# A graph layer with gathered rows: a fifth buffer for rows of x, loaded one stage earlier, paid for by two smaller tiles

## The chip, the cores and the metric

The kernel runs on one core of one Trainium2 chip. The metric is device time in microseconds (us), as the median of several runs. Beside the timed runs there is one execution under the hardware profiler; all engine times, waits and orders in time come from that one.

## The reference

One layer of a graph network over N = 8192 nodes with C = 256 features and E = 131072 edges, sorted by destination:

```
ea   = edge_attr @ w_e + b_e
agg  = segment_sum(relu(x[src] + ea), dst, N)
h_local = bn1(relu((x + agg) @ w1 + b1) @ w2 + b2 + x)
h_attn  = bn2(attention within groups of 32 nodes, 4 heads, out_w + x)
out  = h_local + h_attn
out  = bn3(out + relu(out @ m_w1 + m_b1) @ m_w2 + m_b2)
x    = layernorm(x + out)
```

## The kernel before, in words

**Edges.** The edges are cut into 128 blocks of 1024. For each block POOL issues eight indirect gathers (`gather`, L212 to L228), each of 128 rows of x or, from block 20 on, of xb, a copy of x with b_e added. They land in a tile xs, of which there are six (BUFS). For eight blocks the last gather is replaced by single row loads on SP (`row_stream`, L243, tile xf), so there are 1016 gathers. DVE transposes the edge attributes (eaT, L304), TensorE (PE) multiplies them with w_e (tile pe), DVE adds pe to xs (L363), ACT applies relu in place (L367). DVE builds a one-hot matrix oh from the offsets rel of the edges' destinations within their group (`edge_hot`, L375). PE sums the messages by group with it (tile pw, `pair_sums`), ACT copies a pair's sums to ws (`edge_sums`, L411), and PE places them by a second one-hot oh2 into a window of node columns (tile l, `edge_place`), which DVE adds to xT (L437).

**Nodes.** The 8192 nodes are 16 chunks of 512. A chunk goes through three generators:

- `attention_front` (L583): load the rows of x (`load_nodes`, L442 to L444, tile xn, four buffers), transpose them on PE (L178), copy them to xT and a scaled form to hA on ACT (L594, L595), and make q and k (at<-xT,inT; ACT L608 evacuates).
- `attention_back` (L612): v, the scores, softmax, and the output projection (L690).
- `dense` (L696): two layers on x + agg (w1 with L716, w2 with L720), two more layers on the sum (mw1 with L727, mw2 with L740), then transposes back (zT, L748), the residual with the rows of xn (L754), statistics and normalisation (L756 to L766), and the store (L771). The residual is the last reader of xn.

A front of chunk c may begin when the dense stage of chunk c - 4 has set "dense" (L761), that is, when its rstd is issued. The front first issues its load and yields LOAD, which makes the planner let that stream rest (two turns in the early part, FAR = 10 planned us later on), and only then records the transposes.

**The order.** PE's order is written out by a planner in the kernel: the class `Work` holds four streams (two dense streams, fronts, backs) and hands out pieces of them between edge pieces, by planned times in us. Up to block NV = 24 (`stated`) the orders of DVE and ACT are written out too; behind that the tile framework orders them. SP issues its DMAs in its own order: edge attributes (L267, four buffers), row loads, xn loads, stores. A stage of the back stream sets `after`, and `may` (L892) lets the stream go on only when enough messages have been told; `told` is counted only while `stated` holds.

**The holds.** `hold_fetches` (L189) ties every gather to a PE instruction: gather n waits for the last PE instruction whose planned time is at most n x 1.254 - 10 us, so that gathers don't run ahead of the work.

Of the kernel before, what the change touches and what calls it, by code (L numbers as in the profile page):

```python
# [9 lines left out]
FP = mybir.dt.float32  # L10
I32 = mybir.dt.int32
BF = mybir.dt.bfloat16
# [7 lines left out]
P = 128  # L20
N, C, E, ED, H, NPG = 8192, 256, 131072, 64, 4, 32
# [3 lines left out]
NB = E // BE  # L25
# [3 lines left out]
TB = NH * TJ  # L29
# [5 lines left out]
CH = 512  # L35
NCH = N // CH
BPC = NB // NCH
TN = CH // P
# [42 lines left out]
def window(b):  # L81
    return NPB + 2 * SLACK[b]
# [6 lines left out]
def gnn_kernel(ctx: ExitStack, tc: tile.TileContext, x, src, dst, edge_attr, w, out):  # L89
    nc = tc.nc  # L90

    const = ctx.enter_context(tc.tile_pool(name="const", bufs=1))
# [22 lines left out]
    agg = dram.tile([AGG_ROWS, C], FP, name="agg")  # L115

    srci = const.tile([P, NB, TB], I32, name="srci")
    rel = const.tile([P, NB, TB], FP, name="rel")
    wrow = const.tile([P, NB], FP, name="wrow")
    width = const.tile([1, 1], I32, name="width")  # L120
    we = const.tile([P, C], FP, name="we")
# [30 lines left out]
    epool = fast.enter_context(tc.tile_pool(name="edge", bufs=1))  # L152
# [10 lines left out]
    clock, placed_at = [0.0], [-10.0]  # L163
# [218 lines left out]
    def group_sums(pw, i, b, turns):  # L382
        clock[0] += 0.13 * len(turns)
        for h, j in turns:
            matmul(
                pw[h * WN : (h + 1) * WN, i, :], oh_of[b][:, h * TJ + j, :], msg_of[b][:, h, j, :],
                start=(j == 0), stop=(j == TJ - 1), skip_group_check=True,
            )
# [13 lines left out]
    def edge_sums(blocks):  # L402

        n = len(blocks)
        pw = pw_of.pop(blocks[0], None)
        if pw is None:
            pw = pps.tile([P, 2, C], FP, name="pw", tag="at", bufs=4)
            for i, b in enumerate(blocks):
                group_sums(pw, i, b, [(h, j) for j in range(TJ) for h in range(NH)])
        ws = epool.tile([P, 2, C], FP, name="ws", tag="ws", bufs=2)  # L410
        newest["ws"] = nc.scalar.copy(ws[:, :n], pw[:, :n]).ins  # L411
        oh2 = epool.tile([P, 2, WB], FP, name="oh2", tag="oh2")
        for i, b in enumerate(blocks):
            wn = window(b)
            nc.vector.tensor_scalar(oh2[:, i, :wn], iota_n[:, :wn], wrow[:, b : b + 1], None, ALU.is_equal)
        return blocks, ws, oh2
# [20 lines left out]
            newest["xT"] = nc.vector.tensor_add(xT, l2[:, :, a - n : z - n], xT).ins  # L437

    chunk = [{} for _ in range(NCH)]
    stated = [True]  # L440

    def load_nodes(n0, st, pool):  # L442
        xn = st["xn"] = pool.tile([P, TN, C], FP, name="xn", tag="xn", bufs=4)
        nc.sync.dma_start(xn, x[ds(n0, CH), :].rearrange("(t p) c -> p t c", p=P))  # L444

    with tc.tile_pool(name="setup", bufs=1) as sp:
# [249 lines left out]
    def dense(n0, st, pool, bank, a=0, z=CH, own=("h1", "m1", "zT", "y", "")):  # L696
# [22 lines left out]
        for o in range(KC):  # L719
# [2 lines left out]
            ).ins  # L722
            yield 1.7 * part
        yield NEED
        m1 = pool.tile([P, 2 * KC, w], FP, name="m1", tag=own[1])
        for o in range(2 * KC):
            newest["relu"] = nc.scalar.activation(m1[:, o, :], layer(mw1, KC, o, hA), AF.Relu, bias=v_("m_b1", o)).ins  # L727
# [148 lines left out]
    class Work:  # L876
# [14 lines left out]

        def may(self, i):  # L892
            s = self.streams[i]
            return s and not self.rest[i] and self.told >= self.after[i] and clock[0] >= self.free[i] and s[0][0]()

        def run(self, us):
            self.owed += us
# [57 lines left out]
    with tc.manual_schedule(engines={PE}):  # L955
# [9 lines left out]
        for c in range(NCH):  # L965
            st, before, same = chunk[c], chunk[c - 1], chunk[c - 4]
# [50 lines left out]
        while b < TAIL:  # L1017
# [6 lines left out]
            for i in blocks:  # L1024
                if i + 2 < NB:
                    gather(i + 2)
                if 4 <= i < 8:
                    wt, name = ((w1, "w1"), (w2, "w2"), (mw1, "m_w1"), (mw2, "m_w2"))[i - 4]
# [13 lines left out]
            if stated[0]:  # L1042
# [8 lines left out]
                if waiting:  # L1051
                    pair_sums(1, waiting)
                    sums = edge_sums(waiting)
# [16 lines left out]
            else:  # L1070
                pair_sums(0, waiting)
                edge_products(b)
                pair_sums(1, waiting)
                sums = edge_sums(waiting)
                waiting = list(blocks)
                edge_messages(b)
# [17 lines left out]
        t, l, s = came[b - 2] + 20, b - 2, b - 2  # L1094
# [11 lines left out]
        while l < NB:  # L1106
# [56 lines left out]
            elif t >= times[2]:  # L1163
                i, k = p
# [11 lines left out]
        work.finish()  # L1176
    hold_fetches()
    fast.close()


    wide = nc.values_load(width[0:1, 0:1])
    with tc.If(wide > 0):
        with tc.tile_pool(name="gen", bufs=1) as pool, tc.tile_pool(name="gen_ps", bufs=1, space=PSUM) as ps_pool:
# [11 lines left out]
            with tc.For_i(0, E, P * TE) as e0:  # L1195
# [16 lines left out]
                for j in range(TE):  # L1212
# [17 lines left out]
                    ws = pool.tile([P, C], FP, name="gws", bufs=2)  # L1230
# [19 lines left out]
        with tc.tile_pool(name="gfin", bufs=1) as pool, tc.tile_pool(name="gfin_ps", bufs=1, space=PSUM) as ps_pool:  # L1250
# [7 lines left out]
            with tc.For_i(0, N, CH) as n0:  # L1258
                st = {}
# [42 lines left out]
```

## Time and profile before

| | us |
|---|---|
| median of 3 runs | 1316.11 |
| lowest, highest | 1313.69, 1318.36 |
| the profiled execution's own time | 1310.89 |
| its span, first to last instruction | 1309.1 |
| busy: PE, DVE, ACT, POOL | 1172.2, 800.4, 589.3, 969.2 |
| mean granted PE clock | 0.969 of full speed |
| HBM traffic over the span | 182 GB/s |

A group of instructions has its line, engine, operation, output <- inputs, the count, busy us and mean ns, and the idle time of the engine just ahead of it with what ended that. A timeline row has start and duration in us, engine, line, operation, tiles and count, and in brackets the idle time before it and its releaser. "SPq" is the queue of DMAs that SP issues. A row of waits has the waiter, whom it waited for, the total us, how often, and the longest. A row of windows has the stretch, the busy us of PE, PEld, DVE, ACT and POOL in it (with counts), the granted PE clock, the share of DMA time and GB/s. Matmuls are pipelined and their ends are modelled; an f32 matmul counts as two instructions in the trace and as one in an order.

### The profile page before, as it was taken

The numbers are of one execution on the slowest core, as the hardware profiler recorded it, in microseconds if no ns is written. First come the engines' busy times: TensorE is split into PE (matmuls) and PEld (weight loads), VectorE is DVE, ScalarE is ACT, GpSimd is POOL, SyncE is SP. The second block draws the span as 40 slices with busy tenths as digits, with TensorE's granted clock in tenths as the row PEclk, the third lists the DMA queues.
The fourth block names the chain that finished last, engine by engine and source line by source line (L and its number), as shares of the span: only waits on it lengthen the run. The fifth ranks groups of instructions, "written<-read, shape, count | busy, mean of one in ns | idle before, by whom it ended". The sixth has DMA issues, their size and how long they took to land.

```text
span 1309.1 us, 25348 instructions
## 1 busy us (share of the span) xinstructions
PE 1172.2 (90%) x7591; PEld 698.7 (53%) x7591; DVE 800.4 (61%) x1653; ACT 589.3 (45%) x842; POOL 969.2 (74%) x1024
## 2 busy tenths in 40 slices
PE   4969889899998899879997799899989898999886
PEld 3546455456554555445554455555545455555565
DVE  6676674568664765536667275675646575586653
ACT  2535343455535454344544345454444454543433
POOL 6777777677777777777777777777777777777772
PEclk8999989899999999989999799999999999999999
DMA  8999986758566666565755666676766766666641
GB/s 231 263 332 276 297 233 154 183 148 230 149 167 181 170 185 160 154 186 156 199 160 155 188 171 183 161 201 156 187 175 170 183 171 190 160 175 161 178 118 55
DMA packets 150762, 240.68 MB, mean 184 GB/s; under 512 B 28862, under 2 KB 114268, under 8 KB 149852
## 3 DMA queue, kind: packets, MB, share of 16 engines
q0 software_dynamic: 48768, 133.23, 38.4%
q1 hardware_dynamic: 100764, 105.77, 29.9%
q8 instruction: 62, 1.02, 0.3%
q14 instruction: 80, 0.66, 0.2%
q10 hardware_dynamic: 1088, 0.00, 0.0%
HBM read 222.13 MB, written 16.78 MB: 182 GB/s over the span
## 4 chain that ended last, share of the span: by engine, by line
PE 58%; DMA 15%; issue 8%; DVE 8%; POOL 5%; SPq 3%; ACT 3%; DVEq 0%; ACTq 0%; POOLq 0%
PE at L174 31%; PE pe L174 13%; DMA xs<-xb,srci 8%; PE pw L174 7%; POOL xs L221 5%; PE l L174 3%; DMA ea<-in_edge_attr_dram 3%; DVE xs L363 3%; DMA xn<-in_x_dram 2%; DMA xs<-in_x_dram,srci 1%; SPq L243 1%; SPq L267 1%; DVE bd L666 1%; PE at L797 1%; DVE eaT L304 1%
## 5 line engine op out<-in xcount | busy, mean ns | idle before, releaser
L221 POOL DMA_INDIRECT xs<-xb,srci x856 | 811.8, 948 | 265.0 <-issue 180.1
L367 ACT ACTIVATE xs<-xs 128x1024 f32<-128x1024 f32 (+1 forms) x251 | 261.9, 1046 | 386.6 <-DVE xs L363 355.6
L363 DVE TENSOR_TENSOR xs<-pe,xs 128x1024 f32<-128x1024 f32 (+1 forms) x251 | 296.6, 1205 | 155.1 <-PE pe L174 73.1
L174 PE MATMUL pe<-we,eaT 64*128 64x256 f32 x2048 | 274.0, 402 | 41.9 <-DVE xs L363 31.5
L174 PEld LDWEIGHTS pe<-we,eaT 64*128 64x128 f32 x2048 | 190.6, 192 | 130.5 <-DVE xs L363 42.3
L221 POOL DMA_INDIRECT xs<-in_x_dram,srci x144 | 140.0, 972 | 45.0 <-issue 28.6
L174 PE MATMUL pw<-xs,oh 128*32 128x256 f32 x2048 | 139.1, 391 | 1.6 <-ACT xs L367 1.6
L174 PE MATMUL at<-xT,inT 128*128 128x512 f32 x256 | 125.1, 620 | 9.1 <-DVE hA L720 6.7
L375 DVE TENSOR_TENSOR oh<-iota_n,rel 128x128 f32<-128x128 f32 x256 | 62.4, 280 | 99.7 <-PE pw L174 99.5
L174 PE MATMUL at<-hA,mw 128*128 128x512 f32 (+1 forms) x256 | 115.4, 578 | 0.0
L174 PE MATMUL at<-m,mw 128*128 128x512 f32 (+1 forms) x256 | 110.0, 574 | 2.4 <-DVE xT L437 1.6
L304 DVE STREAM_TRANSPOSE eaT<-ea 128x512 f32<-128x512 f32 x128 | 89.5, 700 | 16.7 <-PE pe L174 13.3
L174 PEld LDWEIGHTS pw<-xs,oh 128*32 128x32 f32 x2048 | 55.7, 110 | 78.6 <-issue 42.6
L174 PEld LDWEIGHTS l<-oh,ws 128*128 128x128 f32 x512 | 72.6, 190 | 33.1 <-issue 20.8
L174 PE MATMUL l<-oh,ws 128*128 128x160 f32 (+4 forms) x512 | 81.6, 298 | 5.3 <-DVE hA L690 3.4
L174 PEld LDWEIGHTS at<-xT,inT 128*128 128x128 f32 x256 | 47.9, 195 | 66.4 <-issue 49.2
L174 PEld LDWEIGHTS at<-m,mw 128*128 128x128 f32 x256 | 47.2, 191 | 52.1 <-issue 48.3
L727 ACT ACTIVATE m<-at,vec 128x512 f32<-128x512 f32 (+1 forms) x64 | 41.7, 656 | 69.1 <-PE at L174 69.0
L174 PEld LDWEIGHTS at<-hA,mw 128*128 128x128 f32 x256 | 46.4, 192 | 44.8 <-issue 37.4
L174 PE MATMUL at<-xT,w 128*128 128x512 f32 (+1 forms) x128 | 59.0, 593 | 9.7 <-DVE xT L437 9.7
L608 ACT ACTIVATE qk<-at,vec 128x512 f32<-128x512 f32 x64 | 43.5, 683 | 50.4 <-PE at L174 49.6
L174 PE MATMUL at<-oT,outT 128*128 128x512 f32 x128 | 61.2, 602 | 2.9 <-ACT oT L681 2.9
(163 smaller groups left out, 1216.4 us busy)
## 6 DMA issues: line engine op xcount, KB each, us to landing
ea<-in_edge_attr_dram SPq DMA_DIRECT2D x512, 128.0 KB
xf<-xb SPq DMA_DIRECT2D x1024, 1.0 KB
xs<-xb,srci POOLq DMA_INDIRECT x856
xn<-in_x_dram SPq DMA_DIRECT2D x16, 512.0 KB
out_dram<-y SPq DMA_DIRECT2D x14, 512.0 KB
xp<-in_x_dram SPq DMA_DIRECT2D x10, 512.0 KB
xb<-xp SPq DMA_DIRECT2D x10, 512.0 KB
xp<-in_x_dram SPq DMA_DIRECT2D x3, 1024.0 KB
```

Source lines behind the costliest of these rows:

```text
L174: mark(ps, nc.tensor.matmul(ps, *args, **kw).ins)
L221: nc.gpsimd.indirect_dma_start(out=xs[:, h, j, :], out_offset=None, in_=x if b < NX else xb[:, :], in_offset=bass.IndirectOffsetOnAxis(ap= ...
L243: nc.sync.dma_start(xf[m * QR + r : m * QR + r + 1, :], xb[ds(row, 1), :])
L267: nc.sync.dma_start(ea[p0 : p0 + QR, c0 : c0 + NH * EQ * ED].rearrange("r (g d) -> r g d", g=NH), edge_attr[b * BE : (b + 1) * BE, :].rear ...
L304: nc.vector.transpose(eaT, ea[:, QR:].rearrange("p (g d) -> p g d", d=ED)[:, :, :QR])
L363: nc.vector.tensor_add(msg[:, hs, js].rearrange("p u i c -> p i u c"), pe[:, js, u : u + n, :], xs[:, hs, js].rearrange("p u i c -> p i u c"),
L367: nc.scalar.activation(msg[:, hs, js], msg[:, hs, js], AF.Relu)
L375: nc.vector.tensor_tensor(oh[:, ts], iota_n[:, None, :WN].to_broadcast([P, TB // 2, WN]), rel[:, b, ts, None].to_broadcast([P, TB // 2, WN ...
L608: nc.scalar.activation(qk[:, o, :], ps, AF.Identity, bias=v_("in_b", o))
L666: nc.vector.transpose(bd[q, :, :, g, :].rearrange("p t h q -> p (t h) q"), pr3[q])
L727: newest["relu"] = nc.scalar.activation(m1[:, o, :], layer(mw1, KC, o, hA), AF.Relu, bias=v_("m_b1", o)).ins
L797: nc.tensor.matmul(ps[i], wt[:, k, o * P : (o + 1) * P], act[:, k, :], start=(k == 0), stop=(k == nk - 1))
```

## The change

It has four parts:

1. xn has five buffers instead of four. The load for chunk c + 4 is issued in the dense stage of chunk c, between the second and the third layer, in the whole-chunk stages of the fast path only. A front whose xn is there already neither loads nor yields LOAD.
2. rel is bf16 instead of f32 (2 KB instead of 4 KB a partition). It holds small whole numbers.
3. ws has one buffer instead of two (2 KB less a partition).
4. In `may`, the condition on `told` holds only while `stated` does.

```diff
-    rel = const.tile([P, NB, TB], FP, name="rel")
+    rel = const.tile([P, NB, TB], BF, name="rel")
...
-        ws = epool.tile([P, 2, C], FP, name="ws", tag="ws", bufs=2)
+        ws = epool.tile([P, 2, C], FP, name="ws", tag="ws")
...
-    stated = [True]
+    stated, fast_path = [True], [True]
...
-        xn = st["xn"] = pool.tile([P, TN, C], FP, name="xn", tag="xn", bufs=4)
+        xn = st["xn"] = pool.tile([P, TN, C], FP, name="xn", tag="xn", bufs=5)
...
         yield NEED
+        if fast_path[0] and not a and n0 // CH + 4 < NCH:
+            load_nodes(n0 + 4 * CH, chunk[n0 // CH + 4], pool)
         m1 = pool.tile([P, 2 * KC, w], FP, name="m1", tag=own[1])
...
-            return s and not self.rest[i] and self.told >= self.after[i] and clock[0] >= self.free[i] and s[0][0]()
+            return s and not self.rest[i] and (self.told >= self.after[i] or not stated[0]) and clock[0] >= self.free[i] and s[0][0]()
...
     fast.close()
+    fast_path[0] = False
```

The planner's decisions move with it. Three places show how. In the rows, at is a PSUM bank of the node work, l that of the placement, pe the edge products, pw the group sums; w_88 is w1, w_89 w2, h_... the tile h1. Lines behind L724 are two higher in the changed kernel.

First place: PE, at the end of chunk 0's dense stage (zT), the start of chunk 1's (w_88) and the front of chunk 4 (xn, inT). Before:

```order
L748 MATMUL at<-ident,zT 128x128 x8
L174 MATMUL l_2006<-oh_1942,ws 128x144 x4
L174 MATMUL at<-xT,w_88 128x512 x2
L178 MATMUL at<-ident,xn 128x128 x8
L174 MATMUL at<-xT,w_88 128x512 x2
L174 MATMUL at<-xT,inT 128x512 x2
L174 MATMUL at<-h_2013,w_89 128x512 x2
L174 MATMUL at<-xT,inT 128x512 x2
L174 MATMUL pe<-we,eaT 128x256 x8
```

Now:

```order
L750 MATMUL at<-ident,zT 128x128 x8
L178 MATMUL at<-ident,xn 128x128 x8
L174 MATMUL l_2016<-oh_1944,ws 128x144 x4
L174 MATMUL at<-xT,inT 128x512 x2
L174 MATMUL at<-xT,w_88 128x512 x2
L174 MATMUL at<-xT,inT 128x512 x2
L174 MATMUL at<-xT,w_88 128x512 x2
L174 MATMUL at<-xT,inT 128x512 x2
L174 MATMUL pe<-we,eaT 128x256 x8
```

The transposes of xn moved ahead of the placement, and a pair for q and k ahead of the first dense layer; the second layer (w_89) moved behind the edge products. On DVE, at the same place, the two additions to xT (L437) moved ahead of the reciprocal and the four scalings of y.

Second place: ACT, at the normalisation of chunk 7 and the front of chunk 11 (rstd is the reciprocal deviation's root, xT and hA the front's two copies). Before:

```order
L760 ACT_TABLE_LOAD
L760 ACTIVATE rstd<-mv,eps_t 128x4
L367 ACTIVATE xs<-xs 128x1024
L716 ACTIVATE h_7998<-at,vec 128x512 x2
L367 ACTIVATE xs<-xs 128x1024
L411 COPY ws<-pw 128x512
L360 ACTIVATE xs<-xs 128x1024
L594 COPY xT<-at 128x512
L595 ACTIVATE hA<-xT,cA,s_99 128x512
L594 COPY xT<-at 128x512
```

Now:

```order
L762 ACT_TABLE_LOAD
L762 ACTIVATE rstd<-mv,eps_t 128x4
L594 COPY xT<-at 128x512
L595 ACTIVATE hA<-xT,cA,s_99 128x512
L594 COPY xT<-at 128x512
L595 ACTIVATE hA<-xT,cA,s_99 128x512
L608 ACTIVATE qk<-at,vec 128x512
```

The copies of xT moved directly behind rstd; four rows of edge messages and of the dense layer that stood between moved behind them.

Third place: PE at the front of the same chunk 11. Before:

```order
L178 MATMUL at<-ident,xn 128x128 x8
L174 MATMUL pe<-we,eaT 128x256 x8
L174 MATMUL at<-h_7998,w_89 128x512 x2
L174 MATMUL at<-xT,inT 128x512 x2
L174 MATMUL at<-h_7998,w_89 128x512 x2
L174 MATMUL l_8205<-oh_8097,ws 128x160 x4
```

Now:

```order
L174 MATMUL pe<-we,eaT 128x256 x8
L750 MATMUL at<-ident,zT 128x128 x8
L178 MATMUL at<-ident,xn 128x128 x8
L174 MATMUL l_7995<-oh_7842,ws 128x160 x4
L174 MATMUL at<-xT,inT 128x512 x2
L174 MATMUL at<-xT,w_88 128x512 x2
L174 MATMUL at<-xT,inT 128x512 x2
```

The transposes of z and of xn stand back to back now, and only one placement is left between xn and the first pair for q and k, where edge products and a dense pair stood.

## The prediction

> **What bounds the kernel now.** I read the profile's page first, for the engines' shares and the slices.
>
> ```profile
> span 1309.1 us, 25348 instructions
> PE 1172.2 (90%) x7591; PEld 698.7 (53%) x7591; DVE 800.4 (61%) x1653; ACT 589.3 (45%) x842; POOL 969.2 (74%) x1024
> POOL 6777777677777777777777777777777777777772
> ...
> PE 58%; DMA 15%; issue 8%; DVE 8%; POOL 5%; SPq 3%; ACT 3%; DVEq 0%; ACTq 0%; POOLq 0%
> ```
>
> TensorE (PE) is the busiest, and the chain of the page goes through it for 58%. But the line to look at is the even row of sevens: POOL issues gathers at one rate from the start to the end. So I read the groups by line next, and then POOL's own timeline, gather by gather.
>
> ```profile
> L221 POOL DMA_INDIRECT xs<-xb,srci x856 | 811.8, 948 | 265.0 <-issue 180.1 <-PE at L174 23.2 <-PE pw L174 15.9
> L221 POOL DMA_INDIRECT xs<-in_x_dram,srci x144 | 140.0, 972 | 45.0 <-issue 28.6 <-DMA xs<-in_x_dram,srci 4.6 <-PE at L174 3.5
> 4.88 1.10 POOL L221 DMA_INDIRECT xs<-in_x_dram,srcd  x1 [3.28 <-issue]
> ...
> 136.59 0.94 POOL L221 DMA_INDIRECT xs<-in_x_dram,srci  x1 [0.67 <-DMA xs<-in_x_dram,srci]
> ...
> 150.65 0.95 POOL L221 DMA_INDIRECT xs<-in_x_dram,srci  x1 [1.09 <-PE at L174]
> ...
> 238.86 0.94 POOL L221 DMA_INDIRECT xs<-xb,srci  x1 [0.30 <-issue]
> 242.00 0.94 POOL L221 DMA_INDIRECT xs<-xb,srci  x1 [2.20 <-PE at L174]
> 245.49 0.94 POOL L221 DMA_INDIRECT xs<-xb,srci  x1 [2.55 <-ACT hA L595]
> 246.74 0.95 POOL L221 DMA_INDIRECT xs<-xb,srci  x1 [0.30 <-issue]
> ...
> 1286.77 0.94 POOL L221 DMA_INDIRECT xs<-xb,srci  x1 [0.30 <-issue]
> ```
>
> The fence's timeline rows give start, duration and, in brackets, the idle time before and its releaser. A gather takes 0.95 us and the next starts 0.30 us later whatever is named in the bracket, so a step is 1.25 us. From the first start (4.88) to the last (1286.77) there are 1015 steps, 1281.9 us, and 1015 x 1.25 = 1268.8. The 13.1 us over are gathers longer than 0.95 (the two groups' means of 948 and 972 hold them) and exactly four gaps above 0.30 in the whole run, the four shown: 0.37 + 0.79 + 1.90 + 2.25 = 5.3 us. What follows the last gather's start takes 1309.1 - 1286.77 = 22.3 us. So the time is 4.9 + 1281.9 + 22.3, POOL sets it, and an edit pays only if it shortens a gather's step, one of the four gaps, or the last 22.3 us. PE time by itself is worth nothing, unless PE is so late that a gather's hold (the PE instruction that it must wait for) has not been reached.
>
> Then the waits on x rows, the thing the change is about: the view of tile xn, and PE's and SP's timeline where PE waits longest.
>
> ```profile
>   DMA xn<-in_x_dram: 43.6, 7
> ...
> PE pe L174 <- DVE xs L363: 31.8, 17, 5.3
> PE at L178 <- DMA xn<-in_x_dram: 22.1, 4, 13.8
> ...
> 721.19 1.55 SPq L243 DMA_DIRECT2D xf<-xb  x4
> 722.84 0.40 SPq L444 DMA_DIRECT2D xn<-in_x_dram  x1
> ...
> 727.73 1.97 PE L178 MATMUL at<-ident,xn 128*128 128x128 f32 x8 [13.83 <-DMA xn<-in_x_dram]
> ...
> 569.96 1.97 PE L178 MATMUL at<-ident,xn 128*128 128x128 f32 x8 [6.06 <-DMA xn<-in_x_dram]
> ...
> 700.00:750.00 50.00, 35.02 (x174) 19.12 (x171) 21.50 (x41) 20.13 (x26) 37.80 (x41) 0.83 0.64 173
> 752.67 1.88 PE L174 MATMUL at<-hA,mw 128*128 128x512 f32 x4
> ...
> 755.46 0.94 POOL L221 DMA_INDIRECT xs<-xb,srci  x1 [0.30 <-PE pw L174]
> ```
>
> The first row counts PE's and its weight load's wait for xn (43.6), the third PE's alone: 22.1 us in four waits. PE's largest wait is another, 31.8 us for the edge messages of DVE. SP issues its queue in order, and the xn load stands behind edge and row loads; at 722.84 it is issued so late that PE stands 13.83 us. Yet in that window POOL still works 37.80 of 50 us with 41 gathers, its full rate: PE had been ahead. Thirty microseconds later PE is hardly in time: the weight pair at 752.67 ends at 754.55, and the gather that comes next starts at 755.46.
>
> **The change part by part.** The early load. Before, a front's xn load is issued when the front begins, after the dense stage of the chunk four back; now it is issued in that stage, two layers and one buffer earlier, and the front begins at once. Every load is still one SP instruction of 0.40 us and the same 512 KB; on SP it moves ahead of edge and row loads, and the row loads of 1.55 us for four lose 0.40 once per chunk, which SP hides. The 22.1 us of PE waiting go. By the sum that buys nothing by itself, since no gather waited in those stretches. What it buys is a margin at the next holds, as at 755.46.
>
> The gaps at 242 and 245 are another matter. They lie at the place that the order shows first: the front of chunk 4 beside the dense stage of chunk 1.
>
> ```profile
> 231.00 1.15 PE L174 MATMUL l<-oh,ws 128*128 128x144 f32 x8
> 232.37 1.28 DVE L754 TENSOR_TENSOR y<-at,xn 128x512 f32<-128x512 f32 x2
> 235.82 0.30 ACT L760 ACTIVATE rstd<-mv,eps_t 128x4 f32<-128x4 f32 x1 [1.97 <-DVE mv L757]
> 236.36 1.38 DVE L766 TENSOR_SCALAR y<-y,mv,rstd 128x256 f32<-128x256 f32 x4
> 237.66 0.65 DVE L437 TENSOR_TENSOR xT<-l,xT 128x80 f32<-128x80 f32 x2
> 237.95 3.78 PE L174 MATMUL at<-xT,w 128*128 128x512 f32 x4 [5.80 <-DVE xT L437]
> 241.52 1.49 PE L178 MATMUL at<-ident,xn 128*128 128x128 f32 x8
> 242.60 0.58 ACT L594 COPY xT<-at 128x512 f32<-128x512 f32 x1
> 242.84 1.88 PE L174 MATMUL at<-xT,w 128*128 128x512 f32 x4
> 243.22 0.81 ACT L595 ACTIVATE hA<-xT,cA,s 128x512 f32<-128x512 f32 x1
> 243.94 0.56 ACT L594 COPY xT<-at 128x512 f32<-128x512 f32 x1
> ```
>
> Before, PE waits 5.80 us for the placed sums (L437), which stand on DVE behind the normalisation of y. Then the layer's first half ends at 241.73 and its second at 244.72, and the two gathers start behind these, at 242.00 and 245.49. After, the xn transposes come ahead of the sums' placement, L437 ahead of the scaling of y, and a pair of q/k products (at<-xT,inT) ahead of the layer. That pair needs both copies of xT, and ACT makes them behind rstd: 235.82 + 0.30, then 0.58, 0.81 and 0.56 with small gaps, about 238.1. With 1.88 for the pair it is done at 240.0, where the first of the two gathers, free at 240.11, is held now; the layer's first half is done at 241.9, where the second, free at 241.35, is held. By these rows 0.5 us remains of the 4.15. If PE starts slowly after its wait, as the 3.78 against 1.88 for the same four matmuls shows it can, 1.90 comes on top, some 2.6 in all. I take 1.2 and a gain of 3.0, with 1.5 and 3.7 as ends. The other two gaps (136.59, 150.65) lie ahead of all that moves and stay.
>
> What is late next. In every front from chunk 4 on the order now has the transposes of z and of xn back to back, and from chunk 8 on ACT's copies of xT directly behind rstd; the second and third places show it. The row nearest to this is the stage at 861, in today's order:
>
> ```profile
> 860.89 1.04 PE L748 MATMUL at<-ident,zT 128*128 128x128 f32 x8
> ...
> 863.48 1.25 PE L174 MATMUL l<-oh,ws 128*128 128x160 f32 x8
> 865.33 0.30 ACT L760 ACTIVATE rstd<-mv,eps_t 128x4 f32<-128x4 f32 x1 [1.92 <-DVE mv L757]
> ...
> 872.13 1.04 PE L178 MATMUL at<-ident,xn 128*128 128x128 f32 x8
> ```
>
> From the start of the z transposes to rstd are 4.7 us, and to the second xT copy some 2.0 more: 6.7. PE's cover is 1.04 for z, 1.04 for xn (872.13) and 1.25 for the sums, 3.3 us. So PE waits about 3 us (at the least 0, where other work slips between; at the most 5) once per front, in 11 fronts behind chunk 4: 33 us. Gone are the 22.1, plus the slow starts behind the two long waits (1.97 for eight xn transposes, 1.04 elsewhere: 0.9 each). PE's total hardly changes; it loses in small pieces what it lost in two large ones. The fronts also stand earlier among the holds: counted in the order, a gather asks for up to eight pairs of 1.88 more PE work than before, 15 us, at about 400 and 560 us. Two things give PE room for that: the 31.8 us that it waits for messages today, where it has nothing else in its order, and the freed 22.1. I take nothing for this, and 0 to 6 us as ends, the upper one from a wait of 5 instead of 3 us in the first three of these fronts.
>
> The rest has one answer each. rel in bf16 touches four casts at the start and the 256 comparisons of L375, 280 ns each and 62.4 us in all; a tenth more or less, 6 us, lies beside DVE's 39% of idle time. One buffer of ws: a copy must wait for the placement matmuls of the pair before, which stand ahead of the sums it copies on PE, so there is nothing to wait for. The relaxed condition in the planner takes effect only where a stage would be stuck. The last 22.3 us keep their order but for single pairs.
>
> ```profile
> L375 DVE TENSOR_TENSOR oh<-iota_n,rel 128x128 f32<-128x128 f32 x256 | 62.4, 280 | 99.7 <-PE pw L174 99.5
> ```
>
> **A rule against it.** The 5.80 us wait is followed by four matmuls in 3.78 us instead of 1.88. The Trainium skill ("TensorE: Matmul & The Clock Gate", Part 1: The HAM clock gate) says that the array falls to half its clock after an idle window of about 3.4 us and needs as long of work to come back; this trace agrees (1.90 us lost; the granted clock was 0.83 in the window with the 13.83 us wait). By that rule the new waits, estimated at 3 us, stay just below the step, and the sum stands as it is. Were they 4 us, the rule would charge each front half of 3.4, about 1.7 us (an estimate from that page's window), 19 us of PE in all.
>
> **The sum.** Profiled execution: 1310.9 us, of which the span is 1309.1. 1310.9 - 3.0 = 1307.9. The median of the three runs, 1316.11, is 5.2 us above that execution, so 1316.1 - 3.0 = 1313.1. This is below what a measurement of this kernel can tell from no change, 0.3% or 3.9 us (the runs themselves span 4.7).
>
> **Rivals.** *The runs' excess goes too.* Nothing in the gathers' steps explains why the timed runs lie 2.8 to 7.5 us above the profiled one, but late PE could: a margin of 0.9 us at 755 is lost if PE restarts a little slower after 13.83 us. Then the early load removes what it costs there: up to 5.2 us beside the 3.0, about 1309. Against it: the profiled run shows no gap there. 0.27.
>
> *The gain is not there.* PE's start after its wait is slow again, or the copies come later still, so that the gaps at 242 and 245 merely move: 1316. What speaks for it is that ACT's copies do hang on the same DVE chain that holds L437 now. 0.17.
>
> *Slower: PE waits for xT at every front.* If the wait is 4 to 5 us rather than 3, each of the 11 fronts also restarts slowly: 11 x (4.5 + 1.9) = 70 us against some 24 freed, so PE loses 46 us net over the 850 us in which its idle time is the room that it has. Today's waits for messages (31.8) absorb most of that; what is left, 14 us, reaches POOL where holds are tight, as at 755: up to 1330, and 1323 with half of it. It decides from a wait of 3.4 us on. Against it: DVE's statistics take only 4 us in the row at 861, and PE has edge products to fill in. 0.13.
>
> **Numbers.** My forecast has 0.43, of which 0.08 falls beyond 0.3%. Faster: 0.27 + 0.08 = 0.35. Within 0.3%: 0.35 + 0.17 = 0.52. Slower: 0.13. The range reaches from 1307 (both gains whole: 1316.1 - 3.7 - 5.2 = 1307.2) to 1320 (the extra PE waits at their 0 to 6 us end, no gain at 242); it leaves out most of the slow case.
>
> **What would show it.** In the profile after: the row of sevens on POOL unchanged; 41 gathers per 50 us; the gaps at 242 and 245 together under 2.7 us; no PE wait on xn above 1 us behind 250 us; a new PE wait of about 3 us for ACT xT L594 once per chunk; L375 within a tenth of 280 ns. I am wrong if POOL shows new gaps above 0.30 between 300 and 1150 us, if the steps themselves are not 1.25, or if the tail behind the last gather moves by more than 2 us.

## The result, and the profile after

The changed kernel is slower: a median of 1386.19 us (1384.13 to 1388.02, four runs) against 1315.18 (1313.69 to 1318.36, four runs), a ratio of 1.0549 with an interval of 1.053 to 1.0568. The forecast was 1313.1, with 1320 as the upper end. The profiled execution took 1384.13 us with a span of 1382.2; its span is 73.1 us longer than that of before. Ratios below are always against runs of the kernel before on the same chip; on two of the chips that kernel itself takes about 1644 us (the last section says what its engines do there).

The page of the changed kernel, its engines, POOL's slices and the chain:

```profile
span 1382.2 us, 25334 instructions
PE 1192.6 (86%) x7591; PEld 714.5 (52%) x7591; DVE 806.7 (58%) x1653; ACT 592.2 (43%) x842; POOL 968.1 (70%) x1024
POOL 6777777777777777777676766767676665746772
...
PE 64%; DVE 14%; DMA 8%; issue 5%; ACT 4%; POOL 2%; SPq 2%; DVEq 0%; ACTq 0%; POOLq 0%
```

No engine has much more to do: PE 20.4 us, DVE 6.3, POOL 1.1 less. But the even row of sevens has holes from the second half on. The groups say how much, and what waits instead:

```profile
L221 POOL DMA_INDIRECT xs<-xb,srci x856 | 812.6, 949 | 337.9 <-issue 185.1
L174 PE MATMUL pe<-we,eaT 64*128 64x256 f32 x2048 | 289.7, 420 | 124.0 <-DVE eaT L304 93.4
L375 DVE TENSOR_TENSOR oh<-iota_n,rel 128x128 f32<-128x128 f32 x256 | 63.3, 281 | 126.6 <-PE pw L174 126.0
```

In the first row the idle time ahead of the gathers is 337.9 us where it was 265.0: 72.9 us more, which is the whole of the 73.1. The gathers themselves are as long as before (949 ns against 948). This one figure, the idle time in that row, is the meter for all that follows. Counted on POOL's timeline, 58 gathers now wait longer than 0.40 us, 79.8 us in all beyond the usual 0.30, where four did, with 5.3. Of the 79.8, 41.4 end at edge products and 17.3 at q and k products. The second row is the new thing: the edge products wait 93.4 us for eaT, the transposed edge attributes that DVE makes (L304). PE's waits:

```profile
PE pe L174 <- DVE eaT L304: 93.4, 30, 7.7
PE pe L174 <- DVE xs L363: 23.0, 9, 5.3
PE at L174 <- ACT xT L594: 15.9, 17, 2.3
PE at L174 <- DVE bd L666: 10.7, 3, 4.0
```

Before, the rows for eaT and xT were these:

```profile
PE pe L174 <- DVE eaT L304: 4.9, 2, 2.6
...
PE at L174 <- ACT xT L594: 2.4, 2, 2.1
```

The wait for xn (22.1) is gone, as the change meant. Here is one of the 30, in the timeline of all engines:

```profile
798.91 2.62 SPq L267 DMA_DIRECT2D ea<-in_edge_attr_dram  x4
...
819.20 2.00 PE L174 MATMUL pe<-we,eaT 64*128 64x256 f32 x16
821.53 0.70 DVE L304 STREAM_TRANSPOSE eaT<-ea 128x512 f32<-128x512 f32 x1
836.38 2.85 DVE L666 STREAM_TRANSPOSE bd<-pr 32x512 f32<-32x512 f32 x4
839.26 0.71 DVE L304 STREAM_TRANSPOSE eaT<-ea 128x512 f32<-128x512 f32 x1
840.12 3.73 PE L174 MATMUL pe<-we,eaT 64*128 64x256 f32 x16 [7.47 <-DVE eaT L304]
842.47 0.95 POOL L221 DMA_INDIRECT xs<-xb,srci  x1 [2.37 <-PE pe L174]
```

The transpose at 839.26 needs edge rows whose last load was issued at about 800 (first row) and a buffer that the products of 819.20 gave back at 821.2. By these two it could have run 18 us earlier: when its rows landed the trace does not tell, but in e10, below, a transpose starts 3.5 us after its last load was issued. It runs directly behind bd, the last step of the softmax, because DVE's order has it there, and bd hangs on a chain that starts with PE's scores. So PE stands for 7.47 us, restarts slowly (3.73 for sixteen products, 2.00 at 819.20), and the next gather, held until these products, starts 2.07 us late. The windows around it, with the granted PE clock in the column behind the five engines:

```profile
836.00:840.00 4.00, 0.00 (x0) 0.00 (x0) 3.87 (x7) 0.70 (x1) 3.09 (x4) 0.60 0.37 111
840.00:844.00 4.00, 3.88 (x17) 2.96 (x18) 1.34 (x2) 0.50 (x1) 1.05 (x2) 0.54 0.78 171
```

DVE is busy for 3.87 of the 4 us in which PE does nothing: an engine with 42% of idle time over the span is the bound here, for a few microseconds. Such a wait comes at 583.0, 668.9, 754.5, 840.1, 925.7, 1012.7 and 1098.8, once in a chunk of eight blocks, and the chunk now takes 85.6 to 87.0 us; at POOL's rate, 64 steps of 1.25, it takes 80. Half of the 79.8 us, 39.9, lies behind 1039 us, where waits for eaT follow one another more closely.

That is not written in the diff, nor in what the planner sets down. It is DVE's order behind block 24, which the tile framework makes. What stands on DVE around the softmax of a chunk near 840 us, before and after:

```
before                                       after
L652 TENSOR_REDUCE mx<-pr 128x16             L652 TENSOR_REDUCE mx<-pr 128x16
L655 TENSOR_TENSOR pr<-pr,mx 128x128 x4      L375 TENSOR_TENSOR oh<-iota_n,rel 128x128
L363 TENSOR_TENSOR xs<-pe,xs 128x2x2x256     L655 TENSOR_TENSOR pr<-pr,mx 128x128 x4
L659 TENSOR_REDUCE sm<-pr 128x16             L363 TENSOR_TENSOR xs<-pe,xs 128x2x2x256 x2
L363 TENSOR_TENSOR xs<-pe,xs 128x2x2x256     L659 TENSOR_REDUCE sm<-pr 128x16
L660 RECIPROCAL sm<-sm 128x16                L375 TENSOR_TENSOR oh<-iota_n,rel 128x128
L304 STREAM_TRANSPOSE eaT<-ea 128x512        L660 RECIPROCAL sm<-sm 128x16
L662 TENSOR_TENSOR pr<-pr,sm 128x128 x4      L375 TENSOR_TENSOR oh<-iota_n,rel 128x128
L666 STREAM_TRANSPOSE bd<-pr 32x16x32 x4     L662 TENSOR_TENSOR pr<-pr,sm 128x128 x4
L740 TENSOR_TENSOR zT<-at,zT 128x512         L666 STREAM_TRANSPOSE bd<-pr 32x16x32 x4
                                             L304 STREAM_TRANSPOSE eaT<-ea 128x512
```

Before, the transpose stands ahead of the last two steps of the softmax; after, behind them. In the whole order eaT stands directly behind bd in seven chunks running, before in one.

### The profile page after: what moved, and what is told of

Same layout as the page of the kernel before. It is cut to its first block, busy times and chain, and to the rows that moved or that the text cites. A ratio compares the mean times of both kernels' runs of the same rounds, so it can differ in the third digit from the quotient of the medians.

```text
span 1382.2 us, 25334 instructions
## 1 busy us (share of the span) xinstructions
PE 1192.6 (86%) x7591; PEld 714.5 (52%) x7591; DVE 806.7 (58%) x1653; ACT 592.2 (43%) x842; POOL 968.1 (70%) x1024
## 4 chain that ended last, share of the span: by engine, by line
PE 64%; DVE 14%; DMA 8%; issue 5%; ACT 4%; POOL 2%; SPq 2%; DVEq 0%; ACTq 0%; POOLq 0%
PE at L174 35%; PE pe L174 16%; PE pw L174 7%; DMA xs<-xb,srci 5%; PE l L174 4%; DVE xs L363 4%; DMA ea<-in_edge_attr_dram 3%; POOL xs L221 2%; DVE bd L666 2%; DVE eaT L304 2%; PE at L799 1%; ACT pr L646 1%; DVE y L756 1%; SPq L243 1%; DVE st L758 1%
## 5 line engine op out<-in xcount | busy, mean ns | idle before, releaser
L221 POOL DMA_INDIRECT xs<-xb,srci x856 | 812.6, 949 | 337.9 <-issue 185.1
L174 PE MATMUL pe<-we,eaT 64*128 64x256 f32 x2048 | 289.7, 420 | 124.0 <-DVE eaT L304 93.4
L174 PEld LDWEIGHTS pe<-we,eaT 64*128 64x128 f32 x2048 | 205.4, 202 | 217.6 <-issue 122.3
L174 PE MATMUL at<-xT,inT 128*128 128x512 f32 x256 | 126.5, 617 | 15.9 <-ACT xT L594 15.9
L375 DVE TENSOR_TENSOR oh<-iota_n,rel 128x128 f32<-128x128 f32 x256 | 63.3, 281 | 126.6 <-PE pw L174 126.0
L174 PE MATMUL at<-hA,mw 128*128 128x512 f32 (+1 forms) x256 | 118.9, 591 | 0.0
L437 DVE TENSOR_TENSOR xT<-l,xT 128x352 f32<-128x352 f32 (+14 forms) x107 | 43.4, 427 | 94.0 <-PE l L174 93.8
L304 DVE STREAM_TRANSPOSE eaT<-ea 128x512 f32<-128x512 f32 x128 | 89.8, 701 | 6.5 <-PE pe L174 3.9
L729 ACT ACTIVATE m<-at,vec 128x512 f32<-128x512 f32 (+1 forms) x64 | 41.9, 657 | 85.7 <-PE at L174 85.6
```

The lines of the kernel that those rows point to most:

```text
L174: mark(ps, nc.tensor.matmul(ps, *args, **kw).ins)
L221: nc.gpsimd.indirect_dma_start(out=xs[:, h, j, :], out_offset=None, in_=x if b < NX else xb[:, :], in_offset=bass.IndirectOffsetOnAxis(ap= ...
L304: nc.vector.transpose(eaT, ea[:, QR:].rearrange("p (g d) -> p g d", d=ED)[:, :, :QR])
L375: nc.vector.tensor_tensor(oh[:, ts], iota_n[:, None, :WN].to_broadcast([P, TB // 2, WN]), rel[:, b, ts, None].to_broadcast([P, TB // 2, WN ...
```

## The experiments

Two theories stood at the start. *Late transposes*: the early load makes the framework order DVE anew, eaT comes late, and PE with it. *Packed fronts*, the slow rival of the prediction: PE's new order, with transposes, copies and q and k back to back, makes PE late at the holds. The expectations speak of both, and of three further rivals: the smaller tiles, the early load itself, and late edge rows (the early loads delay the edge loads on SP's queue).

**The smaller tiles alone** (e1_tiles_only). The kernel before with rel, ws and the fifth buffer, which nothing uses:

```diff
-    rel = const.tile([P, NB, TB], FP, name="rel")
+    rel = const.tile([P, NB, TB], BF, name="rel")
...
-        ws = epool.tile([P, 2, C], FP, name="ws", tag="ws", bufs=2)
+        ws = epool.tile([P, 2, C], FP, name="ws", tag="ws")
...
-        xn = st["xn"] = pool.tile([P, TN, C], FP, name="xn", tag="xn", bufs=4)
+        xn = st["xn"] = pool.tile([P, TN, C], FP, name="xn", tag="xn", bufs=5)
```

> The kernel before with rel in bf16, one ws and a fifth (unused) buffer of xn; no load is moved, and the orders of PE, DVE and ACT stay as before. Theory (late transposes: from block 24 on DVE's order is made by the tile framework, and the early xn loads make it put the transposes of edge attributes, eaT, behind work that waits for PE): 1311 to 1319 us. Rival 'packed fronts' (PE's new order costs the time): the same. Rival 'smaller tiles' (the single ws or the bf16 comparison costs it): 1345 or more.

1315.92 us against 1317.22, ratio 0.9993 (0.9976 to 1.001). The tiles cost nothing.

**The early load with PE's order as before** (e2_early_load_old_pe_order). The changed kernel, but a front whose rows are there rests as if it had loaded them, and the planner writes PE's order word for word as before:

```diff
+        elif n0 >= 4 * CH:
+            yield LOAD
```

> The changed kernel with the front resting after its load as before, so that PE's order is word for word that of the kernel before; the loads stay early. In DVE's order 41 of the blocks from 26 on have an eaT with less than 3 us of PE work between what DVE waits for ahead of it and the product that uses it (the changed kernel has 35, the kernel before 1). Theory (late transposes): 1385 to 1425 us, and PE waits for eaT over 80 us. Rival 'packed fronts': 1311 to 1319 us, as PE's order is the old one. Rival 'late edge rows' (the early loads delay the edge loads on SP's queue itself): 1365 to 1390, with PE's and DVE's waits for ea.

1387.02 us, ratio 1.0551 (1.0517 to 1.0585). Its row of waits and its gathers:

```profile
PE pe L174 <- DVE eaT L304: 110.4, 45, 10.3
```

```profile
L221 POOL DMA_INDIRECT xs<-xb,srci x856 | 813.8, 951 | 336.2 <-issue 177.1
```

As slow as the changed kernel, with 336.2 us ahead of the gathers against 337.9, and no packed fronts. Packed fronts aren't needed for the loss. Late edge rows are not the cause either: behind block 26 every transpose starts 20.4 us or more after its last edge load was issued here, 19.9 in the changed kernel and 20.7 in the kernel before. Row by row in the traces, DVE's order differs from that of before in 650 of 1653 places behind the four casts of rel, and ACT's in 40 of 842; no run below pins the one without the other.

**Transposes ahead, by edges** (e3_transposes_ahead_on_dve). In the changed kernel everything of a block is ordered behind the newest eaT:

```diff
+                with tc.issue_after(newest["eaT"]):
-                work.run(0.35 * per)
-                edge_hot(b + 1)
+                    work.run(0.35 * per)
+                    edge_hot(b + 1)
```

> The changed kernel with DVE's node and one-hot work of blocks 24 to 103 queued behind the eaT that is traced ahead of it. PE's order is the changed kernel's, SP's order nearly so (each edge load stands behind as many row loads, to within 4); in the last 24 blocks eaT stays late. Theory (late transposes): the waits for eaT go from 93 to under 40 us, POOL's gaps before 1100 us nearly vanish and those behind stay in part: 1325 to 1355 us. Rivals 'packed fronts' and 'late edge rows': 1375 to 1390, as neither PE's nor SP's order changes.

1441.33 us, ratio 1.0942 (1.0906 to 1.0978): slower still, which neither theory had. Two rows of PE's waits:

```profile
PE at L174 <- DVE bd L666: 69.9, 10, 7.6
...
PE pe L174 <- DVE eaT L304: 13.6, 7, 4.6
```

The wait for eaT is down to 13.6, but the softmax's bd is 69.9 us late now. The edit moved lateness from one operand to another and tells the theories apart no further.

**Transposes ahead, by priority of their loads** (e4_edge_loads_preferred). In the changed kernel the edge rows' loads get priority from block 28 on:

```diff
+        with tc.high_priority() if b >= 28 else ExitStack():
-        for j in range(TJ):
+            for j in range(TJ):
```

> The changed kernel with the edge loads from block 28 on traced at high priority, so that SP's order has them up to 76 row loads earlier; PE's order is word for word the changed kernel's, and every eaT of DVE's order has at least 11 us of PE work behind it. Theory (late transposes): no PE wait for eaT above 3 us, 1306 to 1318 us. Rival 'packed fronts': 1375 to 1390. Rival 'late edge rows': 1306 to 1318 as well.

1595.95 us, ratio 1.2103 (1.2064 to 1.2142), a clear miss. The wait for eaT is 2.3 us; but what its waits and its timeline show is this:

```profile
PE at L178 <- DMA xn<-in_x_dram: 258.2, 8, 35.9
```

```profile
544.43 24.88 SPq L243 DMA_DIRECT2D xf<-xb  x44
...
569.36 0.41 SPq L445 DMA_DIRECT2D xn<-in_x_dram  x1
...
573.37 1.94 PE L178 MATMUL at<-ident,xn 128*128 128x128 f32 x8 [35.90 <-DMA xn<-in_x_dram]
```

SP issues in order, the 44 single-row loads take 0.565 us each, and the load of x rows stands behind them: the early load itself became late. Yet DVE's and ACT's orders of this kernel have eaT in time, and the next experiments take them.

**Orders written out.** From here on the orders that the framework made are replaced by a table: each instruction of an engine is told to stand behind the one before it on that engine, which adds no wait between engines.

```diff
+    def pin(engine, kinds, order, skip=()):
...
+        for a, z in zip(order, order[1:]):
+            tc.add_manual_dep(
...
+    pin(mybir.EngineType.DVE, ...)
```

The early load with the orders of before (e5_early_load_old_orders, and e8_early_load_old_orders, the same program): the kernel of e2, with DVE, ACT and SP (but for the xn loads) as in the kernel before. It ran first on a chip where the kernel before takes 1643.96 us.

> As the early load with the old PE order, but DVE's, ACT's and SP's orders are pinned to those of the kernel before by a table, SP's but for the xn loads, which stay early. What differs from the kernel before is then only the place of twelve loads on SP (and the smaller tiles). Theory (late transposes): 1306 to 1317 us; PE waits neither for xn nor for eaT. Rival 'the early load itself' (the 512 KB or their place on SP's queue delay other transfers): 1360 to 1390.

> The same program as e5, for a trace without the halts of all engines that e5, e6 and e7 show. Theory (late transposes): no PE wait for xn or eaT above 3 us, POOL's gaps above 0.30 us under 6 us in all, 1307 to 1316 us, so between 0.2% slower and 0.7% faster than the kernel before. If the early load is worth more than the four gaps (the rival of the prediction that late PE costs the timed runs 5 us): 1309 or less.

There, 1625.88 us, ratio 0.9894 (0.9866 to 0.9922). On an undisturbed chip, 1315.09 against 1315.76, ratio 0.9998 (0.9979 to 1.0018). The gathers of the latter:

```profile
L221 POOL DMA_INDIRECT xs<-xb,srci x856 | 812.6, 949 | 266.2 <-issue 174.0
```

266.2, as before (265.0). The gaps were expected under 6 us and are 9.0, still four, all ahead of 250 us. The rival that the early load is worth more (1309 or less) falls. Early load, fifth buffer, smaller tiles: all that the diff names is in this kernel, and it costs nothing and gains nothing. All of the 71 us comes from orders.

The changed kernel with its own PE and SP orders, and DVE's and ACT's from e4 (e6_changed_kernel_repinned and e9_changed_kernel_repinned, the same program; e13_repinned_control ran it a third time):

> The changed kernel, PE's and SP's orders word for word its own, with DVE's and ACT's pinned by a table to those that came out where the edge loads were preferred: every eaT from block 26 on has 11 us or more of PE work behind it. Theory (late transposes on DVE alone): PE's wait for eaT goes from 93 to under 5 us and the time to 1306 to 1320. Rivals 'packed fronts' and 'the early load itself': 1370 to 1390, as PE's and SP's orders are the changed kernel's.

> The same program as e6, for a trace without the halts. Theory (late transposes): PE waits for eaT under 5 us, 1306 to 1320 us; if the packed fronts cost something of their own, it is what this stands above e8. Rivals 'packed fronts' and 'the early load itself' as the main cause: 1370 to 1390.

On the chip of e5, 1646.65 us, ratio 1.0013 (0.9989 to 1.0036). Undisturbed, 1335.58 us, ratio 1.0146 (1.0124 to 1.0168). PE's waits in the latter, and its gathers:

```profile
PE at L174 <- DVE bd L666: 35.9, 10, 4.2
...
PE at L174 <- ACT xT L594: 17.2, 13, 2.3
```

```profile
L221 POOL DMA_INDIRECT xs<-xb,srci x856 | 812.5, 949 | 288.9 <-issue 174.6
```

With eaT in time (2.3 us of waits, one) 51 of the 71 us are gone, by the medians 1386.19 - 1335.58. Some 20 stay, more than the 1320 expected allows. The packed fronts are in part of it: of the 31 gaps above 0.40 us, with 31.4 us beyond 0.30, 14 with 11.1 us end at q and k products or their copies. Here are two gaps of one front on POOL's timeline:

```profile
794.24 0.94 POOL L221 DMA_INDIRECT xs<-xb,srci  x1 [1.02 <-PE at L174]
...
798.89 0.94 POOL L221 DMA_INDIRECT xs<-xb,srci  x1 [1.21 <-ACT qk L608]
```

**Late transposes alone** (e7_old_loads_late_transposes). The other way round: the kernel before with the smaller tiles, late loads and PE's own order, and DVE and ACT pinned to the orders of e2; on the chip of e5.

> The kernel before (with the smaller tiles), its loads of xn late as they were and PE's order its own, with DVE's and ACT's orders pinned to those of the early load with the old PE order, in which 41 blocks have an eaT with under 3 us of PE work behind it. Theory (late transposes): 1380 to 1410 us, PE waits for eaT 90 to 130 us. Rivals 'packed fronts' and 'the early load itself': 1311 to 1319.

1742.78 us, ratio 1.0597 (1.0562 to 1.0632), and in the waits:

```profile
PE pe L174 <- DVE eaT L304: 148.5, 37, 9.5
```

No early load and no packed front, and the loss is there. The microseconds hold the halts of that chip and can't be set beside those that were expected; on the same chip the early load with the orders of before has no wait for eaT and a ratio of 0.9894 (e5). The late loads are in this run too: PE waits 37.9 us for xn, in seven waits. DVE's and ACT's orders suffice for a loss of the changed kernel's size.

**What makes the framework do it** (e10_loads_preferred_only). The kernel before, with priority for the xn load behind block 24 and nothing else:

```diff
-        nc.sync.dma_start(xn, x[ds(n0, CH), :].rearrange("(t p) c -> p t c", p=P))
+        with tc.high_priority() if not stated[0] else ExitStack():
+            nc.sync.dma_start(xn, x[ds(n0, CH), :].rearrange("(t p) c -> p t c", p=P))
```

> The kernel before with one edit: the xn loads behind block 24 are traced at high priority, so that SP's order has them 2 to 6 edge blocks earlier. Buffers, PE's order and all else as before; DVE's order then has 41 blocks with an eaT under 3 us ahead of its product, 1 before. Theory (late transposes, set off by where the framework sees the xn loads): 1375 to 1400 us, PE waits for eaT over 80 us and for xn under 10. Rivals: 1311 to 1319.

1414.42 us, ratio 1.0732 (1.0698 to 1.0765), a little more than expected.

```profile
PE pe L174 <- DVE eaT L304: 131.2, 46, 10.3
```

DVE's order here is that of e2, row by row behind the casts of rel, and so is ACT's: one load per chunk that stands earlier in SP's order is enough to make it. But the time is not that order's alone. With four buffers SP comes to the load before its buffer is free (the wait ends at DVE's residual, the last reader of xn, just ahead of st), and the edge loads stand behind it. SP's and DVE's waits:

```profile
SPq L445 <- DVE st L757: 175.6, 12, 26.8
```

```profile
DVE eaT L304 <- DMA ea<-in_edge_attr_dram: 16.1, 8, 3.8
```

In 7 of the 46 waits of PE for eaT, with 42.4 of the 131.2 us, DVE itself was waiting for a load. So late edge rows are in this run, and the 27 us by which it stands above e2 are not DVE's order, which is the same. By what rule the framework turns the place of a load into DVE's order, no run here shows.

**Looser holds.** If gathers wait only because they are held too closely to PE, looser holds should give the time back. The constant is AHEAD in hold_fetches, 10 us before.

The kernel of e8 with 13 (e11_early_load_looser_holds):

> As e8, with the holds of the gathers 3 us looser (AHEAD 13 instead of 10), so that a gather waits for a PE instruction planned 3 us earlier. POOL's four gaps above 0.30 us (5.3 us in the kernel before) should shrink to under 2 and the time to 3 to 5 us under that of e8. If gathers that run ahead collide with other transfers, it is no faster than e8.

1313.84 us against 1315.76, ratio 0.999 (0.9974 to 1.0006): if there is a gain, it is too small to be told from none. Four gaps stay, with 6.7 us (9.0 in e8), not under 2, and the 3 to 5 us are not there.

The kernel of e9 with 20 (e12_repinned_looser_holds), again on a chip where the kernel before takes 1643.29 us:

> As e9 (the changed kernel with DVE's and ACT's orders pinned so that no eaT is late, 1.5% slower than the kernel before), with the holds of the gathers 10 us looser (AHEAD 20 instead of 10); the orders of PE, DVE, ACT and SP stay word for word those of e9. Theory (the fronts, packed earlier in PE's order, make the holds ask for PE work that isn't there yet, 31 us of POOL's gaps in e9): gaps under 12 us and 1308 to 1322 us. Rival (PE is late in itself: its waits for bd and xT, 53 us in e9, hold back the messages and so the tiles that the gathers fill): gaps stay above 20 us and the time above 1328.

1720.53 us, ratio 1.046 (1.0418 to 1.0502). This answers nothing about the fronts, since most of the loss comes ahead of them. Two waits of POOL's timeline:

```profile
238.39 0.95 POOL L221 DMA_INDIRECT xs<-in_x_dram,srci  x1 [10.49 <-ACT xs L367]
...
302.98 0.95 POOL L221 DMA_INDIRECT xs<-xb,srci  x1 [11.03 <-PE pw L174]
```

The first gather of xb starts at 302.98; in e6, the same program with 10 and on such a chip too, it started at 262.31. That is 40.7 of the 67.2 us by which this span is longer (1722.0 against 1654.8); the other 26.5 come behind it, and no run here shows why. So the looser hold was set to the later gathers alone (e14_repinned_late_looser_holds), beside e13 on the same undisturbed chip:

```diff
-            while i < len(marks) and marks[i][0] <= n * 1.254 - AHEAD:
+            while i < len(marks) and marks[i][0] <= n * 1.254 - (AHEAD if n < 250 else 2 * AHEAD):
```

> The same program as e9, as the measure for e14 on the same chip. Both theories: 1.3 to 1.6% slower than the kernel before where the engines don't halt, about the same as it where they do (e6).

> As e13, with the holds 10 us looser from gather 250 on (320 us); the start, at which e12 lost some 40 us, keeps them. PE's, DVE's, ACT's and SP's orders are word for word those of e13. Theory (the holds ask for the packed fronts' PE work too early): 0.8 to 1.6% faster than e13, with POOL's gaps behind 320 us under 8 us (26 in e9). Rival (PE late in itself): within 0.4% of e13, the gaps wait for free tiles or messages instead.

1326.53 us (ratio 1.0093, 1.0069 to 1.0118) against 1334.5 for e13 (1.0155, 1.013 to 1.0179). Its gathers:

```profile
L221 POOL DMA_INDIRECT xs<-xb,srci x856 | 812.8, 950 | 276.3 <-issue 182.3
```

8 of the 21.5 us that the repinned kernel had lost come back through the holds: between 245 and 1039 us no gather waits any more. That is 0.6%, between the two expectations, and the gaps behind 320 us are 12.8 us, not under 8: the holds are a part and not the whole. 13.5 us stay, their gaps all behind 1039 us but for four at the start, and PE's rows for bd and xT are word for word those of e9. That PE itself is late by then, through these waits and the slow starts behind them, is argued from the rows, not shown by a run of its own; four of the ten gaps behind 1039 us have "issue" in the bracket, which names no engine.

## Why the prediction was wrong, point by point

**The bound.** Right: POOL sets the time, step by step, and the loss is read in one row of it. The first gather starts at 4.71 and the last, in the timeline after, here:

```profile
1359.81 0.94 POOL L221 DMA_INDIRECT xs<-xb,srci  x1 [0.30 <-issue]
```

Behind it are 1382.2 - 1359.81 = 22.4 us, as predicted for the tail (22.3). Nothing but the gaps changed. (Of the 13.1 us above 1015 steps of 1.25, the four gaps are 5.3 and the longer gathers about 4; the rest is the rounding of the step.) Gaps between 300 and 1150 us were named as what would prove the forecast wrong.

**The early load, and the waits for xn.** Right: they go, and by themselves they are worth nothing (e8). With that the rival that the runs' excess goes too is out: e8 is at 1315.09, not about 1309. On the chip of e5 the same program gains 1.1%; whether that is the margin that the waits' going was to buy, no run shows.

**The small edits.** Right: L375 takes 281 ns, predicted within a tenth of 280, and e1 is the same as before.

**The gaps at 242 and 245.** Wrong: 3.0 us were to be gained, 0.24 were. PE's and POOL's timelines after:

```profile
237.16 3.78 PE L174 MATMUL at<-xT,inT 128*128 128x512 f32 x4 [2.28 <-ACT xT L594]
240.73 2.97 PE L174 MATMUL at<-xT,w 128*128 128x512 f32 x4
```

```profile
241.21 0.95 POOL L221 DMA_INDIRECT xs<-xb,srci  x1 [2.20 <-PE at L174]
244.47 0.95 POOL L221 DMA_INDIRECT xs<-xb,srci  x1 [2.31 <-ACT h L716]
```

The q and k products start at 237.16, 0.8 us sooner than the layer did, as the order said, but four take 3.78 us and the next four 2.97 instead of 1.88. Before, the gaps had brackets of 2.20 and 2.55; after, 2.20 and 2.31. The term was mis-sized by the slow start; it is the rival "the gain is not there", at its place.

**What is late next: the step that failed.** The prediction took "nothing for this, and 0 to 6 us as ends"; the idle time ahead of the gathers grew by 72.9. (Its upper end does not add up either: 1316.1 and 6 are 1322, not 1320.) It had the right question and looked for the answer at one place, the fronts, on PE and ACT. There its estimate, 3 us of waiting for xT in each of 11 fronts, was too high: 17 waits, 15.9 us in all, none above 2.3. What it had counted as cover was what came late: "PE has edge products to fill in", against the slow rival, and "DVE's 39% of idle time", against the longer comparisons. The edge products need eaT, and eaT stood on DVE behind a softmax that needs PE: PE waited 93.4 us for it, where it had waited 4.9. The order of DVE behind block 24 was there to be compared before the run, and the prediction spoke of DVE's order at one place only, near 237 us. The missing term is 51 us by the run with eaT put in time (e9), and the whole loss where PE's order is the old one (e2 against e8): the shares of the two causes do not add up. The traces let one see why: in e9 PE waits 3.3 to 4.2 us for bd once in a chunk, where the changed kernel waits about 7.5 us for eaT.

**The slow rival.** It had the sign and, in part, the mechanism. Its price, up to 14 us on top, compares with the 19.8 us of e9, but two things in it were off. The wait for xT is not the larger part there: PE's waits for bd are (35.9 us in ten waits; in the changed kernel itself 10.7 in three), and DVE's order in e9 is that of e4, so not all of the 19.8 need be the fronts'. And it "decides from a wait of 3.4 us on", while PE started slowly after 2.23 us in e9. PE's timeline comes first, then two windows of 3.41 us with PE's busy time in front and the granted clock behind the five engines:

```profile
709.74 3.61 PE L174 MATMUL at<-xT,inT 128*128 128x512 f32 x4 [2.23 <-ACT xT L594]
```

```profile
706.55:709.96 3.41, 1.18 (x9) 0.94 (x8) 3.01 (x13) 2.34 (x5) 2.50 (x4) 1.00 0.36 95
709.96:713.37 3.41, 3.41 (x5) 1.30 (x5) 1.90 (x7) 1.86 (x3) 0.39 (x1) 0.50 0.65 215
```

The Trainium skill ("TensorE: Matmul & The Clock Gate", Part 1: The HAM clock gate) has the step behind an idle window of about 3.4 us. In this trace PE worked for 1.18 of the 3.41 us before 709.96, and still the granted clock was 0.50 in the next 3.41, with 3.61 us for four matmuls that take 1.88 elsewhere; so the measurement decides, and a wait below 3.4 us isn't safe by itself.

## What to carry to other kernels

A load that moves on one queue can move work on engines that the diff never names, wherever a framework and not the author orders them: compare the order of every engine over the whole length before pricing, and above all that of the engine that makes the bound engine's operands. There count how long ahead of its use an operand is made, not how idle its maker is; a DVE that is idle 42% of the time held PE for 93 us. To find the cause among many moved rows, pin the known order of some engines and leave the others (here DVE and ACT together; each alone would have told more); repairs by priority or by edges (e3, e4) only moved the lateness elsewhere, at 4 to 15% more.

## What the runs showed of the hardware that had not been expected

**The same program takes 1316 us on most chips here and 1644 us on two.** That is the kernel before. On those two, stretches are frequent in which all four engines stand still together. One of them in e5, with the busy time of PE, its weight loads, DVE, ACT and POOL:

```profile
716.03:717.09 1.06, 0.01 (x1) 0.00 (x0) 0.00 (x0) 0.00 (x0) 0.00 (x0) 1.00 0.40 101
```

A stretch like this could be a common wait. But e5 has 103 above 0.3 us, 77 us in all, and the same program on an undisturbed chip (e8) has seven, with 3.4; and 238 gathers of e5 wait longer than 0.40 us, 318.8 us in all beyond 0.30, where in e8 four do, with 9.0. The cause isn't to be seen in these traces. Ratios to the kernel before are other there: the early load with the old orders gains 1.1% on that chip (e5) and nothing on an undisturbed one (e8). What the changed kernel's PE order, with DVE's and ACT's from e4, costs on top is nearly the same on both: e6 stands 1.3% above e5, e9 1.6% above e8.

**A slow start depends on where a wait lies, and not on its length alone.** In the changed kernel's timeline on PE, a wait of 7.47 us is followed by sixteen products in 3.73, and one of 1.49 by sixteen in 2.00; a wait of 2.28 is followed by four matmuls at half speed (3.78), and in e9 ten waits of 3.3 to 4.2 us for bd are followed by the same 32 matmuls in anything from 1.97 to 3.51:

```profile
424.85 1.97 PE L174 MATMUL at<-bd,vn 128*64 128x128 f32 x32 [3.38 <-DVE bd L666]
...
668.65 3.39 PE L174 MATMUL at<-bd,vn 128*64 128x128 f32 x32 [3.38 <-DVE bd L666]
```

The same wait, 3.38 us, and 1.42 us between them. The granted clock in the trace of e9 tells them apart. It changes only at moments that are whole multiples of 3.41 us apart (it falls at 669.00, 709.96 and 750.92, each 12 x 3.413 behind the other), and every low stretch is 3.41, 6.83 or 10.24 us long. Cut into these steps of 3.41 us, the two places look like this:

```profile
419.83:423.24 3.41, 1.63 (x4) 0.38 (x2) 3.40 (x9) 1.96 (x3) 2.50 (x4) 1.00 0.84 199
423.24:426.65 3.41, 1.80 (x32) 1.73 (x32) 3.35 (x5) 1.11 (x3) 2.50 (x4) 1.00 0.88 285
...
665.59:669.00 3.41, 0.35 (x6) 0.35 (x8) 3.34 (x6) 1.63 (x2) 2.76 (x3) 1.00 0.93 238
669.00:672.41 3.41, 3.41 (x31) 3.08 (x28) 1.47 (x2) 1.96 (x3) 2.50 (x4) 0.50 0.72 224
```

The first wait lies across two steps, PE is busy for about half of each (1.63 and 1.80 us), and the clock stays at 1.00. The second lies in one, PE is busy for 0.35 us of it, and the clock of the next is 0.50. In all of e9 behind 30 us, with the clock at 1.00, it fell after every step in which PE was busy for less than 0.47 of it and after none with more than 0.50. Where the steps lie against the program differs between executions: in e13, the same program, the first of the two places has a wait of 3.33 us, the clock falls at 426.19, and the 32 matmuls take 2.75 us instead of 1.97.
